# A block of four transformer layers: dummy products for TensorE, a new order of the first steps, and a shorter normalisation on GpSimd

## The chip, the cores and the metric

The kernel runs on one core of a Trainium2 chip. A core has five engines that run side by side and meet through semaphores: PE (TensorE, matrix products and transposes into PSUM), DVE (VectorE), ACT (ScalarE, table functions and scaled copies), POOL (GpSimd) and SP (SyncE, which here issues nearly all DMA transfers). PEld is the loading of a product's stationary operand. The metric is the device time of one execution in microseconds (us); lower is better. The time before is 1635.87 us, the median of three runs (1634.98 to 1640.96).

## The reference, cut to what matters

The input x has 128 sequences of 64 tokens with 128 channels in float32, with one condition vector of 128 channels per sequence and a context of 64 tokens per sequence. Four layers follow each other; the change touches the start of the first one and the normalisation of all.

```python
def _ln(x):
    mu = jnp.mean(x, axis=-1, keepdims=True)
    var = jnp.var(x, axis=-1, keepdims=True)
    return (x - mu) * jax.lax.rsqrt(var + EPS)
...
# layer 0
mod = jax.nn.silu(t_emb) @ adaln_w + adaln_b
sh_sa, sc_sa, g_sa, sh_ff, sc_ff, g_ff = jnp.split(mod[:, None, :], 6, axis=-1)
xm = _ln(x) * (1.0 + sc_sa) + sh_sa
qkv = (xm @ qkv_w + qkv_b).reshape(B, N, 3, H, HD)      # 16 heads of 8
...
x_sa = _attend(q, k, v) @ sa_proj_w + sa_proj_b         # softmax(q k / sqrt(8)) v
x = x + g_sa * x_sa
...                                                     # cross attention to the context, then an MLP
x = x + g_ff * x_ff
```

Layer 1 is a cross attention, layer 2 again self attention, cross attention and MLP, and layer 3 a small attention to the context with a gated mixture of three experts.

## The kernel before, in words

The 8192 tokens are held on the chip as 16 groups of 512 (`xs[s]`, 128 partitions x 4 x 128); a group is 8 sequences. All weights and groups are loaded once by SP in the order in which the program names them (L76 to L117). The order of the instructions on each engine is written out by hand (`stages`); no scheduler moves anything.

An attention runs over the 16 groups in half steps: step `k` computes the scores of half `k%2` of group `k//2`. I number the score products by their step: scores 0 and 1 are those of group 0, scores 2 and 3 of group 1, and so on. One step on PE is: scores of this step (`sc`, L470), transposes of the last step's shifted scores (`pp`, L495), products of the step before that with the values (`po`, L512), and between them pieces of the preparation of later groups and the finish of earlier ones. On DVE a step is a maximum over the scores (`mx`, L477) and their difference to it (`e`, L479); ACT takes the exponential (`eT`, L499). There is one PSUM tile for the scores, so scores k+1 wait until `e` of step k has read it.

`prepare` is the preparation of one group, cut by `yield` into pieces; `ahead_1(i)` runs the next piece of group i. For self attention the pieces are: (1) nothing, (2) mean and variance on DVE (L312, L314) and 1/sqrt on POOL (`rs`, L321 and L322, a power), (3) the normalised `xn` (`normed_by_pool`: a negated mean `nmu` on POOL at L361, then four instructions at L364, on POOL, for the first group on DVE), (4) transposes on PE (`psT`, L334) and the modulation `xm` (eight instructions, one per sequence: for the first group on DVE at L349, otherwise on ACT at L351), (5) nothing, (6) the keys (`pk` L428, `kT` L430) and their copies masked by head (`kbd`, L436, on POOL, for the first group on DVE), (7) the queries (`pq` L441, `qT` L443), (8) the values (`pvv` L451) into a block tile `vbd` (L456, L457). Two `vbd` tiles are cleared once on POOL by `clear` (L171 to L173).

`condition` transposes the condition (`pc`, L245), takes its silu on ACT (`scT`, L247, with a load of ACT's function table ahead of it) and transposes the bias rows (`pv`, L249, `vec`, L250). `first_mods` are three lists of products for the six modulation tables (`pm` L195, additions L199). In the MLPs the modulation is made by `modulated`: one multiplication of the whole tile on DVE (L339) and one addition on POOL (L340), ahead of the first MLP product (`ph`, L675). `first_tables` makes a table of gates (`gb` L219, `pg` L224, `gate_rows` L225, a DMA at L226) and a folded bias (`bvs` L233, `pb` L237, L238). Small PSUM tiles come from the pool `mm`, which has two buffers.

Of the kernel before, what the change touches and what calls it, by code (L numbers as in the profile page):

```python
# [9 lines left out]
F32 = mybir.dt.float32  # L10
AF = mybir.ActivationFunctionType
ALU = mybir.AluOpType
# [3 lines left out]
P = 128  # L16
NST = 16
TT = 4
NB = 8
L = 64  # L20
# [39 lines left out]
def tile_kernel(ctx: ExitStack, tc: tile.TileContext, a: dict, out: bass.AP):  # L60
    nc = tc.nc
    V, S, G, T = nc.vector, nc.scalar, nc.gpsimd, nc.tensor
# [3 lines left out]
    def const(shape, name):  # L66
        return cp.tile(shape, F32, tag=name, name=name)

    x_d = a["x"].rearrange("b n c -> (b n) c").rearrange("(s t p) c -> s p t c", t=TT, p=P)
# [2 lines left out]
    out_d = out.rearrange("b n c -> (b n) c").rearrange("(s t p) c -> s p t c", t=TT, p=P)  # L72


    cond = const([P, P], "cond")
    nc.sync.dma_start(cond, a["cond_1024"])  # L76
    vec_rows = const([_NVEC, P], "vec_rows")
# [13 lines left out]
                nc.sync.dma_start(t, src.rearrange("(k p) n -> p k n", p=P))  # L91
                w[name] = t

    xs = [const([P, TT, P], f"x{s}") for s in range(NST)]

    def load_groups(which):
        for s in which:
            nc.sync.dma_start(xs[s], x_d[s])

    load_groups((0,))  # L100
    load_weights(("L0_xcond_adaln", "L0_xcond_qkv"))
    load_groups((1,))
    load_weights("L0_xcond_sa")
# [3 lines left out]
    for name, n in (("L0_xcond_ca_proj_b", P), ("L1_xcond_bp", P), ("L2_xcond_b_cproj", P), ("L3_xcond_router_b", 3)):  # L107
        t = const([P, n], name)
# [11 lines left out]
    make_identity(nc, ident)  # L120
    nhalf = const([P, TT], "nhalf")
    G.memset(nhalf, -0.5)

    stack, attention_stack = ExitStack(), ExitStack()
    dp = ctx.enter_context(tc.tile_pool(name="dp", bufs=1, space=bass.MemoryType.DRAM))
# [34 lines left out]

    def mm(name):
        return pools[1].tile([P, 512], F32, tag="mm", name=name)

# [4 lines left out]
    def clear(t):  # L170
        G.memset(t, 0.0)  # L171
        G.memset(t[0:L, :, :, 16:17], 1.0)
        G.memset(t[L:P, :, :, 17:18], 1.0)  # L173
# [69 lines left out]
    def condition():  # L243
        pc = mm("pc")
        T.transpose(pc[:, :P], cond, ident)  # L245
        V.tensor_copy(condT, pc[:, :P])
        S.activation(scT, pc[:, :P], AF.Silu)  # L247
        pv = mm("pv")
        T.transpose(pv[:, :_NVEC], vec_rows, ident[:_NVEC, :_NVEC])  # L249
        V.tensor_copy(vec, pv[:, :_NVEC])  # L250
        V.tensor_scalar_add(vec1, vec, 1.0)

    first_mods = modulations("L0_xcond_adaln_w", "L0_xcond_adaln_b", 6, (1, 4))
# [41 lines left out]
    def mod(name, i, s):  # L295

        return mods[name][:, i, ts(s, NB)].unsqueeze(2).broadcast_to([P, NB, L])

    def by_batch(t):
        return t.rearrange("p (b l) -> p b l", b=NB)  # L300
# [29 lines left out]
    def transposed(psum, src):  # L330

        ps = psum.tile([P, 512], F32, tag="mm", name="psT")
        for t in range(TT):
            T.transpose(ps[:, ts(t, P)], src[:, t, :], ident)  # L334
        return ps

    def modulated(pool, ps, name, scale, shift, s, tag="xm"):
        xm = pool.tile([P, NT], F32, tag=tag, name=tag)
        V.tensor_tensor(by_batch(xm), by_batch(ps), mod(name, scale, s), ALU.mult)  # L339
        G.tensor_tensor(by_batch(xm), by_batch(xm), mod(name, shift, s), ALU.add)  # L340
        return xm

    def modulated_by_batch(pool, ps, name, scale, shift, s, tag="xm", by_dve=False):
        xm = pool.tile([P, NT], F32, tag=tag, name=tag)
        for b in range(NB):
            k = NB * s + b
            m, p = (mods[name][:, i, k : k + 1] for i in (scale, shift))
            if by_dve:
                V.tensor_scalar(xm[:, ts(b, L)], ps[:, ts(b, L)], m, p, ALU.mult, ALU.add)  # L349
            else:  # L350
                S.activation(xm[:, ts(b, L)], ps[:, ts(b, L)], AF.Identity, bias=p, scale=m)  # L351
        return xm


# [2 lines left out]


    def normed_by_pool(pool, src, mv, rs, tag, engine=G):
        nmu = pool.tile([P, TT], F32, tag="nmu" + tag, name="nmu")  # L360
        G.tensor_scalar(nmu, mv[:, :, 0], -1.0, 0.0, ALU.mult, ALU.add)  # L361
        xn = pool.tile([P, TT, P], F32, tag=tag, name=tag)
        for t in range(TT):
            engine.tensor_scalar(  # L364
                xn[:, t, :], src[:, t, :], nmu[:, t : t + 1], rs[:, t : t + 1], ALU.add, ALU.mult
            )
        return xn

# [9 lines left out]
    def prepare(pools, at):  # L378

        pool, psum = pools[:2]  # L380
        s, layer = at["s"], at["layer"]
        eps = 1e-5 if layer == "L1c" else 1e-6
        cross = layer[2] == "c"
        if cross:
            c = pool.tile([P, TT, P], F32, tag="c", name="c", bufs=3)
            nc.sync.dma_start(c, ctx_d[s])
        yield
        if layer == "L1c":
            mv = x_mv[:, s]
            rs = inv_std(pool, mv, eps)  # L390
        else:
            mv, rs = stats_of(pool, xs[s], eps)
        yield
        xn = normed_by_pool(pool, xs[s], mv, rs, "xn", V if at.get("first") else G)
        if cross:
            cn = c
            if layer != "L0c":
                cn = pool.tile([P, TT, P], F32, tag="cn", name="cn", bufs=1)
                for t in range(TT):
                    rs, nb = (v[eps][:, s, t : t + 1] for v in (ctx_rs, ctx_nb))  # L400

                    if layer == "L1c":
                        G.tensor_scalar(cn[:, t, :], c[:, t, :], rs, nb, ALU.mult, ALU.add)
                    else:
                        S.activation(cn[:, t, :], c[:, t, :], AF.Identity, bias=nb, scale=rs)
        yield
        if layer == "L1c":
            kv_in = modulated_by_batch(pool, transposed(psum, cn), "L1_xcond_Wss_kv", 0, 1, s, "cm")
        elif cross:
            kv_in = copied(pool, transposed(psum, cn), "cm")  # L410
            if layer == "L0c":
                nc.sync.dma_start(ctxT[s], kv_in)
        else:
            q_in = kv_in = modulated_by_batch(
                pool, transposed(psum, xn), at["wmod"], 1, 0, s, by_dve=at.get("first", False)
            )
        yield
        if not cross:
            pass
        elif layer == "L1c":  # L420
            q_in = modulated(pool, transposed(psum, xn), "L1_xcond_Wss_q", 0, 1, s)
        else:
            q_in = copied(pool, transposed(psum, xn), "xm")
        yield


        pk = psum.tile([P, 512], F32, tag="mm", name="pk")
        T.matmul(pk, at["wk"], kv_in, start=True, stop=True)  # L428
        kT = pool.tile([P, NT], F32, tag="kT", name="kT")
        S.activation(kT, pk, AF.Identity, bias=at["bk"])  # L430
        i = turn[0] % 2
        turn[0] += 1
        vbd = vbds[i]
        kbd = pool.tile([P, 4, NB, L], F32, tag="kbd", name="kbd")
        for j in range(4):
            (V if at.get("first") else G).tensor_scalar(  # L436
                kbd[:, j], by_batch(kT), mask[:, j : j + 1], 1.0, ALU.mult, ALU.mult
            )
        yield
        pq = psum.tile([P, 512], F32, tag="mm", name="pq")  # L440
        T.matmul(pq, at["wq"], q_in, start=True, stop=True)  # L441
        qT = pool.tile([P, NT], F32, tag="qT", name="qT")
        S.activation(qT, pq, AF.Identity, bias=at["bq"])  # L443
        at.update(qT=qT, kbd=kbd)
        yield

        wv_pair = at["wv"].rearrange("p (i j d) -> p j i d", j=2, d=HD)
        pvv = psum.tile([P, NB, L], F32, tag="mm", name="pvv")
        for b in range(NB):
            for j in range(2):  # L450
                T.matmul(  # L451
                    pvv[ts(j, L), b, :], kv_in[:, ts(b, L)], wv_pair[:, j],
                    start=True, stop=True,
                )
        pv4 = pvv.rearrange("p b (i d) -> p b i d", d=HD)
        S.copy(vbd[0:L, :, :, 0:HD], pv4[0:L])  # L456
        S.copy(vbd[L:P, :, :, HD : 2 * HD], pv4[L:P])  # L457
        at["vbd"] = vbd
# [712 lines left out]

    def stages():
        ats = [attention_of(s, layer) for layer in ("L0s", "L0c") for s in groups]
        ats[0]["first"] = True
        ahead_1, steps_1 = attend(pools, ats)
        ahead_2, steps_2 = attend(
            pools, [attention_of(s, layer) for layer in ("L1c", "L2s", "L2c") for s in groups]
# [33 lines left out]
            return turns[last - 1 :]  # L1211


        clear(vbds[0])
        ahead_1(0, 1, 2, 3)
        condition()
        ahead_1(0, 0)
        first_mods[0]()
        ahead_1(0, 0, 1, 2, 0, 0, 1)
        psum_for_attention()  # L1220

        steps_1[0]([lambda: ahead_1(2), lambda: clear(vbds[1]), lambda: ahead_1(1, 1, 0, 3)])
        tables = first_tables()
        steps_1[1]()
        first_mods[1]()
        steps_1[2]()
        for f in tables[:3]:
            f()
        steps_1[3]((), tables[3:])
        for f in steps_1[4:6]:  # L1230
            f()
        first_mods[2]()
        n = last + 2 + len(heads_0)
        for f in steps_1[6:-n]:
# [38 lines left out]
    with tc.manual_schedule():  # L1273
        stages()
# [30 lines left out]
```

## Time and profile before

| | |
|---|---|
| median of three runs | 1635.87 us |
| the profiled execution, its own time | 1636.9 us |
| its span, first to last instruction | 1635.1 us |
| PE busy | 1581.5 us, 97% of the span |
| DVE, POOL, ACT busy | 1296.4, 1079.4, 1038.6 us |
| PE busy in the stretches 0-20, 20-40, 40-60 us | 11.14, 15.78, 18.55 us |
| PE busy in 60-80 us and in 460-520 us | 19.48 of 20, 60.0 of 60 us |
| `nmu` (L361) | 128 instructions on POOL, median 0.193 us |
| `xn` (L364) | 508 on POOL, mean 0.452 us |

Times in a profile are microseconds from the start of the span, unless marked ns. A group row or timeline row gives start, duration, engine, line, operation, output tile and inputs; a float32 product appears as two passes on PE (a count of x2 is one product). The chain is followed back from the last instruction: at each step to what released it, or to the instruction before it on its engine. A busy PE is not PE at its peak: matrix products are pipelined and their ends are modelled.

### The profile page before, as it was taken

To read this page: it belongs to the slowest core of one execution; us is meant where nothing else is said; L and a number is where in the kernel's file an instruction comes from. 1 tells how busy PE (TensorE), PEld (TensorE's weight loads), DVE (VectorE), ACT (ScalarE), POOL (GpSimd) and SP (SyncE) were. 2 spreads that over 40 slices of the span, in tenths; PEclk is the share of its full clock that TensorE was granted. 3 is DMA by queue.
4 is the path that set the end of the run, shared out by engine and by line. 5 is a ranking of instruction groups with operands and counts; after the bars stand their busy time and mean duration, and the time that the engine had idled before them with its cause. 6 is when DMAs were issued, how large, how long until landed. Compare 5 with 4: busy or idle time off the path is not lost.

```text
span 1635.1 us, 64936 instructions
## 1 busy us (share of the span) xinstructions
PE 1581.5 (97%) x27842; PEld 1090.9 (67%) x27842; DVE 1296.4 (79%) x2430; ACT 1038.6 (64%) x1714; POOL 1079.4 (66%) x1814
## 2 busy tenths in 40 slices
PE   6999999998999899999999999998999999999998
PEld 4677767776554467777777677776777666666665
DVE  6999989999566688899999999998454566666666
ACT  5778767776333587788887888886334544444443
POOL 5688777775899888986787786665876333333322
PEclk9999999999999999999999999999999999999999
DMA  7333443322202012211333432221432111111100
GB/s 208 82 93 85 109 118 87 93 81 60 62 27 58 27 47 72 63 47 47 95 86 92 102 99 62 72 56 53 125 91 77 31 37 40 39 34 33 36 11 20
DMA packets 146783, 112.71 MB, mean 69 GB/s; under 512 B 36357, under 2 KB 125247, under 8 KB 146495
## 3 DMA queue, kind: packets, MB, share of 16 engines
q1 hardware_dynamic: 146288, 108.53, 25.0%
q8 instruction: 219, 3.59, 0.9%
q14 instruction: 69, 0.57, 0.1%
q10 hardware_dynamic: 207, 0.03, 0.0%
HBM read 83.99 MB, written 14.02 MB: 60 GB/s over the span
## 4 chain that ended last, share of the span: by engine, by line
PE 79%; DVE 13%; ACT 3%; POOL 2%; issue 1%; DMA 1%; SPq 1%; POOLq 0%; DVEq 0%
PE sc L470 9%; PE pp L495 9%; PE po L512 7%; PE ph L1062 6%; PE ph L675 6%; PE ph L1063 6%; DVE mx L477 5%; DVE e L479 5%; PE po L1093 5%; PE psT L334 5%; PE pk L428 5%; PE py L554 4%; PE py L691 3%; PE pvv L451 3%; PE pq L441 3%; PE py L681 2%
## 5 line engine op out<-in xcount | busy, mean ns | idle before, releaser
L499 ACT ACTIVATE eT<-pp 128x1024 f32<-128x1024 f32 x320 | 329.8, 1030 | 162.5 <-PE pp L495 162.5
L477 DVE TENSOR_REDUCE mx<-sc 128x32 f32<-128x2048 f32 x160 | 366.6, 2291 | 61.8 <-PE sc L470 61.8
L479 DVE TENSOR_TENSOR e<-sc,mx 128x2048 f32<-128x2048 f32 x160 | 366.6, 2291 | 5.4
L495 PEld LDWEIGHTS pp<-ident,e 64*128 64x128 f32 x5120 | 185.1, 139 | 142.6 <-ACT eT L499 46.7
L436 POOL TENSOR_SCALAR kbd<-kT,mask 128x512 f32<-128x512 f32 x316 | 212.4, 689 | 44.0 <-ACT kT L430 41.2
L495 PE MATMUL pp<-ident,e 64*128 64x64 f32 x5120 | 228.9, 229 | 8.4 <-DVE e L479 4.7
L364 POOL TENSOR_SCALAR xn<-x,nmu,rs 128x128 f32<-128x128 f32 x508 | 223.0, 452 | 13.3
L548 POOL TENSOR_TENSOR oT<-o,rb 128x512 f32<-128x512 f32 x80 | 102.0, 1275 | 153.1 <-DMA rb<-recs 65.8
L470 PE MATMUL sc<-kbd,qT 32*64 32x256 f32 x5120 | 181.7, 391 | 16.2 <-DVE e L479 15.3
L676 ACT ACTIVATE h<-ph,vec 128x512 f32<-128x512 f32 x128 | 87.4, 688 | 153.1 <-PE ph L675 152.9
L512 PE MATMUL po<-eT,vbd 128*32 128x64 f32 x10240 | 178.6, 222 | 1.2 <-issue 1.2
L1069 ACT ACTIVATE h<-h 128x512 f32<-128x512 f32 x112 | 70.5, 630 | 148.0 <-DVE h L1065 129.1
L512 PEld LDWEIGHTS po<-eT,vbd 128*32 128x32 f32 x10240 | 152.1, 110 | 14.0 <-issue 1.7
L322 POOL TENSOR_TENSOR rs<-rs,nhalf 128x4 f32<-128x4 f32 x128 | 130.3, 1018 | 10.6
L470 PEld LDWEIGHTS sc<-kbd,qT 32*64 32x64 f32 x5120 | 98.3, 132 | 53.5 <-DVE e L479 19.3
L1065 DVE TENSOR_TENSOR h<-ph,ab 128x512 f32<-128x512 f32 x112 | 77.0, 688 | 55.7 <-PE ph L1063 55.5
L312 DVE BATCH_NORM_STATS2 st<-x 128x6 f32<-128x128 f32 x512 | 110.5, 278 | 0.6
L1098 DVE SCALAR_TENSOR_TENSOR acc<-po,pr,acc 128x128 f32<-128x128 f32 x192 | 67.3, 350 | 44.1 <-PE po L1093 39.5
L1062 PE MATMUL ph<-nx,w 128*128 128x512 f32 x192 | 99.9, 602 | 0.0
L520 ACT COPY o<-po 128x512 f32<-128x512 f32 x160 | 95.7, 598 | 5.7 <-PE po L512 3.5
L1063 PE MATMUL ph<-u,w_ev 128*128 128x512 f32 x192 | 98.0, 592 | 0.0
L1093 PEld LDWEIGHTS po<-w_2o,h 128*128 128x128 f32 x768 | 92.1, 192 | 8.7 <-issue 8.4
(261 smaller groups left out, 2851.8 us busy)
## 6 DMA issues: line engine op xcount, KB each, us to landing
rb<-recs SPq DMA_DIRECT2D x80, 256.0 KB
c<-in_ctx_dram SPq DMA_DIRECT2D x64, 256.0 KB
o<-o SPq DMA_DIRECT2D x320, 32.0 KB
gt<-gate_L_xcond_sa_proj_w SPq DMA_DIRECT2D x32, 256.0 KB
gt<-gate_L_xcond_W_proj SPq DMA_DIRECT2D x32, 256.0 KB
gt<-gate_L_xcond_W_mlp SPq DMA_DIRECT2D x32, 256.0 KB
x<-in_x_dram SPq DMA_DIRECT2D x16, 256.0 KB
ctxT<-cm SPq DMA_DIRECT2D x16, 256.0 KB
```

The costliest lines, as they stand in the source:

```text
L322: G.tensor_tensor(rs, rs, nhalf, ALU.pow)
L364: engine.tensor_scalar(xn[:, t, :], src[:, t, :], nmu[:, t : t + 1], rs[:, t : t + 1], ALU.add, ALU.mult)
L436: (V if at.get("first") else G).tensor_scalar(kbd[:, j], by_batch(kT), mask[:, j : j + 1], 1.0, ALU.mult, ALU.mult)
L470: T.matmul(sc[ts(h, L), g, ts(t2, 256)], qT[ts(g, 32), ts(b, L)], kbd[ts(g, 32), :, b, :], start=True, stop=True,)
L477: V.tensor_reduce(mx, sc.rearrange("p g (m k) -> p (g m) k", k=L), AX.X, ALU.max)
L479: V.tensor_tensor(e, sc.rearrange("p g (m k) -> p (g m) k", k=L), mx.unsqueeze(2).broadcast_to([P, 32, L]), ALU.subtract,)
L495: T.transpose(pp[:, h, ts(4 * g2 + 2 * i + t2, L)], e6[ts(h, L), 2 * gg + g2, t2, i], ident[ts(h, L), ts(h, L)],)
L499: S.activation(eT[:, gg], pp, AF.Exp, scale=HD ** -0.5)
L512: T.matmul(po[ts(g, 32), i, ts(2 * t2 + h, L)], at["vbd"][:, 4 * u + 2 * t2 + h, 2 * g + i, :], e7[:, g // 2, h, g % 2, i, t2, :], start=T ...
L1062: T.matmul(ps, wn, d["nx"], start=True, stop=False)
L1063: T.matmul(ps, we, d["u"], start=False, stop=True)
L1093: T.matmul(po[:, ex, :], d[q][:, ts(t, P)], k3["w_2o"][:, q, :], start=r == 0, stop=r == 1)
```

## The change

The change has these parts.

- **Dummy products.** A tile `busy` of ones is set on DVE. `keep_busy(n)` multiplies it with itself n times into a tile that nothing reads. It is called with 8 ahead of everything on PE, with 4 after `condition`, with 2 after the first modulation products, and with 4 after the first group's transposes.
- **First loads.** The first group of x is loaded ahead of the condition on SP's queue.
- **Order of the first steps.** The first group's statistics come ahead of `condition`; the first modulations come ahead of `xn` on DVE; the first `clear` comes after `rs` on POOL.
- **Exponential's table.** An exponential of a 128x4 tile, which nothing reads, follows the silu, so that ACT's table for it is loaded there.
- **Modulation by whole tiles.** For group 0 the eight instructions at L349 become one multiplication and one addition of 128x512, both on DVE; for group 2 the eight at L351 on ACT become a multiplication on DVE and an addition on POOL.
- **Set-up parts spread.** The second list of modulations moves from before step 2 to after it, and the folded bias from step 3 to step 5.
- **Normalisation.** `nmu` is gone in all layers: `xn` is (x - mean) * rs in one instruction, with the mean read from the statistics.

```diff
@@ -72,6 +72,13 @@
     out_d = out.rearrange("b n c -> (b n) c").rearrange("(s t p) c -> s p t c", t=TT, p=P)
 
 
+    xs = [const([P, TT, P], f"x{s}") for s in range(NST)]
+
+    def load_groups(which):
+        for s in which:
+            nc.sync.dma_start(xs[s], x_d[s])
+
+    load_groups((0,))
     cond = const([P, P], "cond")
     nc.sync.dma_start(cond, a["cond_1024"])
     vec_rows = const([_NVEC, P], "vec_rows")
@@ -91,13 +98,6 @@
                 nc.sync.dma_start(t, src.rearrange("(k p) n -> p k n", p=P))
                 w[name] = t
 
-    xs = [const([P, TT, P], f"x{s}") for s in range(NST)]
-
-    def load_groups(which):
-        for s in which:
-            nc.sync.dma_start(xs[s], x_d[s])
-
-    load_groups((0,))
     load_weights(("L0_xcond_adaln", "L0_xcond_qkv"))
     load_groups((1,))
     load_weights("L0_xcond_sa")
@@ -120,6 +120,9 @@
     make_identity(nc, ident)
     nhalf = const([P, TT], "nhalf")
     G.memset(nhalf, -0.5)
+    nhalf2 = const([P, TT], "nhalf2")
+    busy = const([P, P], "busy")
+    V.memset(busy, 1.0)
 
     stack, attention_stack = ExitStack(), ExitStack()
     dp = ctx.enter_context(tc.tile_pool(name="dp", bufs=1, space=bass.MemoryType.DRAM))
@@ -161,6 +164,12 @@
     def mm(name):
         return pools[1].tile([P, 512], F32, tag="mm", name=name)
 
+    def keep_busy(n):
+
+        p = mm("pi")
+        for _ in range(n):
+            T.matmul(p[:, 0:P], busy, busy, start=True, stop=True)
+
 
 
     vbds = [
@@ -245,6 +254,8 @@
         T.transpose(pc[:, :P], cond, ident)
         V.tensor_copy(condT, pc[:, :P])
         S.activation(scT, pc[:, :P], AF.Silu)
+
+        S.activation(nhalf2, nhalf, AF.Exp)
         pv = mm("pv")
         T.transpose(pv[:, :_NVEC], vec_rows, ident[:_NVEC, :_NVEC])
         V.tensor_copy(vec, pv[:, :_NVEC])
@@ -334,21 +345,18 @@
             T.transpose(ps[:, ts(t, P)], src[:, t, :], ident)
         return ps
 
-    def modulated(pool, ps, name, scale, shift, s, tag="xm"):
+    def modulated(pool, ps, name, scale, shift, s, tag="xm", engine=G):
         xm = pool.tile([P, NT], F32, tag=tag, name=tag)
         V.tensor_tensor(by_batch(xm), by_batch(ps), mod(name, scale, s), ALU.mult)
-        G.tensor_tensor(by_batch(xm), by_batch(xm), mod(name, shift, s), ALU.add)
+        engine.tensor_tensor(by_batch(xm), by_batch(xm), mod(name, shift, s), ALU.add)
         return xm
 
-    def modulated_by_batch(pool, ps, name, scale, shift, s, tag="xm", by_dve=False):
+    def modulated_by_batch(pool, ps, name, scale, shift, s, tag="xm"):
         xm = pool.tile([P, NT], F32, tag=tag, name=tag)
         for b in range(NB):
             k = NB * s + b
             m, p = (mods[name][:, i, k : k + 1] for i in (scale, shift))
-            if by_dve:
-                V.tensor_scalar(xm[:, ts(b, L)], ps[:, ts(b, L)], m, p, ALU.mult, ALU.add)
-            else:
-                S.activation(xm[:, ts(b, L)], ps[:, ts(b, L)], AF.Identity, bias=p, scale=m)
+            S.activation(xm[:, ts(b, L)], ps[:, ts(b, L)], AF.Identity, bias=p, scale=m)
         return xm
 
 
@@ -357,12 +365,10 @@
 
 
     def normed_by_pool(pool, src, mv, rs, tag, engine=G):
-        nmu = pool.tile([P, TT], F32, tag="nmu" + tag, name="nmu")
-        G.tensor_scalar(nmu, mv[:, :, 0], -1.0, 0.0, ALU.mult, ALU.add)
         xn = pool.tile([P, TT, P], F32, tag=tag, name=tag)
         for t in range(TT):
             engine.tensor_scalar(
-                xn[:, t, :], src[:, t, :], nmu[:, t : t + 1], rs[:, t : t + 1], ALU.add, ALU.mult
+                xn[:, t, :], src[:, t, :], mv[:, t, 0:1], rs[:, t : t + 1], ALU.subtract, ALU.mult
             )
         return xn
 
@@ -411,9 +417,13 @@
             if layer == "L0c":
                 nc.sync.dma_start(ctxT[s], kv_in)
         else:
-            q_in = kv_in = modulated_by_batch(
-                pool, transposed(psum, xn), at["wmod"], 1, 0, s, by_dve=at.get("first", False)
-            )
+            first = at.get("first", False)
+            if first or at.get("second", False):
+                q_in = kv_in = modulated(
+                    pool, transposed(psum, xn), at["wmod"], 1, 0, s, engine=V if first else G
+                )
+            else:
+                q_in = kv_in = modulated_by_batch(pool, transposed(psum, xn), at["wmod"], 1, 0, s)
         yield
         if not cross:
             pass
@@ -1171,7 +1181,7 @@
 
     def stages():
         ats = [attention_of(s, layer) for layer in ("L0s", "L0c") for s in groups]
-        ats[0]["first"] = True
+        ats[0]["first"] = ats[2]["second"] = True
         ahead_1, steps_1 = attend(pools, ats)
         ahead_2, steps_2 = attend(
             pools, [attention_of(s, layer) for layer in ("L1c", "L2s", "L2c") for s in groups]
@@ -1211,24 +1221,30 @@
             return turns[last - 1 :]
 
 
+        keep_busy(8)
+        ahead_1(0, 1, 2, 3)
+        ahead_1(0)
+        condition()
+        keep_busy(4)
+        first_mods[0]()
+        keep_busy(2)
+        ahead_1(0)
         clear(vbds[0])
-        ahead_1(0, 1, 2, 3)
-        condition()
-        ahead_1(0, 0)
-        first_mods[0]()
-        ahead_1(0, 0, 1, 2, 0, 0, 1)
+        ahead_1(0)
+        keep_busy(4)
+        ahead_1(0, 1, 2, 0, 0, 1)
         psum_for_attention()
 
         steps_1[0]([lambda: ahead_1(2), lambda: clear(vbds[1]), lambda: ahead_1(1, 1, 0, 3)])
         tables = first_tables()
         steps_1[1]()
+        steps_1[2]()
         first_mods[1]()
-        steps_1[2]()
         for f in tables[:3]:
             f()
-        steps_1[3]((), tables[3:])
-        for f in steps_1[4:6]:
-            f()
+        steps_1[3]((), tables[3:4])
+        steps_1[4]()
+        steps_1[5]((), tables[4:])
         first_mods[2]()
         n = last + 2 + len(heads_0)
         for f in steps_1[6:-n]:
```

## The prediction

> **What bounds the kernel now.** I read the busy shares first, then PE's busy time and clock by stretch, then the chain of waits from the start, then PE's waits.
>
> ```profile
> PE 1581.5 (97%) x27842; PEld 1090.9 (67%) x27842; DVE 1296.4 (79%) x2430; ACT 1038.6 (64%) x1714; POOL 1079.4 (66%) x1814
> ```
> ```profile
> 0.00:20.00 20.00, 11.14 (x82) 6.04 (x82) 11.41 (x46) 4.01 (x8) 11.51 (x28) 1.00 0.92 242
> 20.00:40.00 20.00, 15.78 (x326) 10.45 (x324) 15.77 (x28) 16.26 (x35) 11.63 (x22) 0.91 0.68 183
> ...
> 60.00:80.00 20.00, 19.48 (x482) 13.99 (x482) 18.95 (x20) 16.54 (x33) 16.66 (x27) 1.00 0.38 96
> ```
>
> PE is idle 54 us in all (1635.1 - 1581.5), and 14.5 of these lie in the first 60 us (20-11.14, 20-15.78, 20-18.55). From 60 us on the first attention runs at its own pace: scores start at 62.84, 68.83, 74.77, 80.76, so 5.97 us a step, in which PE's own work and the loop scores, `mx`, `e` (1.12 + 2.29 + 2.29 and the hand-overs) are both nearly full. The change can therefore gain at the start, and what it gains there is carried to the end unless a later stall absorbs it. The chain of waits in the start:
>
> ```profile
> 7.05 0.19 POOL nmu L361
> ...
> 9.02 2.12 DVE xm L349 x8
> ...
> 11.18 2.09 PE pk L428 x2
> ...
> 15.83 2.01 PE sc L470 x32
> ...
> 23.21 2.48 ACT xm L351 x8
> 25.70 1.28 ACT L499
> 27.00 1.03 ACT eT L499
> ...
> 30.14 1.15 PE pm L195 x4
> 31.29 1.92 PE sc L470 x32
> 33.23 2.30 DVE mx L477
> ...
> 43.88 0.44 DVE gate_rows L225
> ```
>
> Three things are to be seen. The first products run at half rate: `pk` takes 2.09 us at 11.18 and 1.12 at 21.45, scores 0 take 2.01 and later ones 1.12. Scores 2 start at 31.29, although `e` of step 1 had left the PSUM tile at 28.94: before them stand the modulation of group 2 and the table load on ACT, which hold the exponential until 27.00 and so the second `pp`, `pvv` and `pm` on PE; the wait was long enough that PE is slow again:
>
> ```profile
> 19.00:29.40 10.40, 6.91 (x126) 1.00 1.04 276
> 29.40:33.00 3.60, 3.60 (x53) 0.53 0.91 252
> ```
> ```profile
> PE ph L675 <- POOL xm L340: 2.5, 3, 1.2
> ```
>
> The columns of the first are stretch, length, PE busy and its instructions, granted clock, DMA share and GB/s. The last is a PE wait outside the start that POOL ends: 2.5 us in three waits, in the MLP of layer 0.
>
> **The change, to the end of scores 0 (17.84 before).** *Dummies.* A dummy is two passes of 128x128; eight such passes took 2.00 us at half rate (`py` at 409.94) and 1.05 at full rate (60.63), so a dummy is about 0.46 or 0.23 us. `busy` is set at about 0.9, so eight dummies fill PE from 1.05 to 4.75 if slow. Their cover: before, PE waited until 3.09 and for the adaln weights until 5.64. The condition now lands behind x, where x landed before (4.38), so `pc` is put off from 3.09 to 4.75. `condT`, `vec` and `scT` (0.29, 0.21, 0.28) end at about 5.85. The next four dummies wait for `vec`, whose PSUM buffer they take, and `pm` stands behind them: the added wait in this step. They end at 7.65 if slow, 6.7 if fast; `pm` could have run at 5.9. Behind `pm` wait the first modulations and now, on DVE, `xn`.
>
> *When does PE get fast?* By the rows, PE became fast in `pvv` at 18.82, 3.0 us after its last pause (15.70), and again at 33.0, 3.6 us of unbroken work after 29.40. [...] But before, `pk` and `pq` were busy 3.8 us from 11.18 to 14.96 and did not do it. So both ends:
> - fast during the four dummies (6.2): `pm` 6.9 to 7.55, modulations (0.61) 8.2, `xn` (1.12) 9.4, `psT` 9.6, `xm` 0.69 + 0.63 by the rows L339 and L559 in place of 2.11, so 11.05; `pk` fast 12.2, `kT` 12.9; DVE must first measure groups 1 and 2 (2.1, as before), so `kbd` (1.68) 13.25 to 14.9; scores 0 end at 16.15: 1.7 us gained. At best (the clock up within the first eight) 2.0.
> - slow until about 11: `pm` ends at 8.6, `xm` at 12.3 (before 11.13, so later), the last four dummies end about there, `pk` is fast; scores 0 end at 17.4: 0.45 gained.
> I take 1.7: eight dummies without a pause are nearest to the rows with 3.0 and 3.6 us.
>
> *Free edits.* The early x lands 0.45 us sooner and `nmu` saves 0.2 + 0.1 us, but `xn` waits for DVE's modulations until 8.2 and `rs` is there at 6.6, so both are hidden. The moved `clear` (2.2 us) lies on POOL at 6.6 to 8.8, ahead of `rs` of group 1, whose variance comes at 12; it would cost only beyond 3 us. SP issues the same transfers, two exchanged; none is moved past another queue. The silent exponential and its load (1.28) lie on ACT at 5.9 to 7.5; ACT is next wanted at 12.2.
>
> **From scores 0 to `mx` 2** (15.39 us before, 17.84 to 33.23). After: `mx`, `e` 4.7; then DVE measures group 3 (1.2) and multiplies for group 2 (0.7), which is new on DVE between two steps and covers scores 1; `mx`, `e` 4.6; scores 2 (1.12) beside the measuring of group 4 (1.25): 12.6 in sum. Is PE ready then? ACT goes from `kT` straight to `eT` (the 2.48 of `xm` and 1.28 of the load are gone), so `pp`, `pq`, `pp`, `pvv` end at about 26, and `pm` has moved; `e` 1 ends at 27.45. Is `kbd` 1? POOL: `rs` of group 3 to 23.5, `kbd` 26.2, then the new addition 1.04 and `xn` of group 3 to 29.1, wanted by PE at 32: covered by 1.2 and 3 us. Gain 2.8, in which the table counts by its row: `xm` ended at 25.69, the load ran 25.70 to 26.98, and `eT` began at 27.00. [...]
>
> **From `mx` 2 to `mx` 6** (24.94 before). `pb` no longer waits for `gate_rows` (44.36 against 43.75, where scores 4 could go): 0.7 gained at `mx` 4. The folded bias (0.34 on PE) and its addition (0.29) now stand with the third modulations ahead of scores 6: 0.6 lost there. Sum 0, from -0.7 to +0.7.
>
> **`nmu` elsewhere.** 128 x (0.193 + about 0.1 to the next start) is 37 us of POOL, nearly all of it where PE or DVE bounds. At the MLP of layer 0 POOL runs without a pause (`xm` L340 at 427.05 and 434.88: 7.83 us a turn), and PE waits for it 1.18, 0.69 and about 0.6 us. One, two and one `nmu` of 0.29 go ahead of these: at most 1.1, at least 0.3 if the waits move; I take 0.6. That subtracting costs POOL what adding a negated mean did is not shown by a row; the nearest is `cn` (L403, other operations, 1.74 for four against 1.73), so I take no difference.
>
> **Sum.** 1.7 + 2.8 + 0 + 0.6 = 5.1 us. The span goes from 1635.1 to 1630.0. The profiled execution took 1636.9, 1.0 over the median; taken off the median, 5.1 us give **1630.8 us**, 0.31% less. About 0.5% (8.2 us) is what a measurement of this kernel can tell from no change, so the forecast lies inside it.
>
> **Rivals.**
> - *The dummies come too late* (PE slow until 11 us and slow again before scores 0, where it idles 1.8 us): 0.45, or -0.5 with slow scores, plus 2.8, and 0.3 for `nmu`: 1633.0. For it: the 3.8 us at 11.18 that did not help. Against it: the dummies are denser.
> - *POOL was worth more*: from 420 to 460 and 520 to 600 us PE is idle 1.9 + 4.8 + 1.7 = 8.4 us. If POOL's shorter turn ends half of that, 4.2 takes the place of 0.6: gain 8.7, 1627.2. For it: POOL without a pause there. Against it: at 545 to 560 PE waits for DVE and `e`, by the chain.
> - *Slower: subtracting is dear on POOL.* In the MLP of layer 0 POOL's turn becomes 7.54 + 4p against PE's 8 x 0.86 + 0.60 + 0.60 + 0.44 = 8.5, p being the extra of one normalisation. It decides from p = 0.24 us. At p = 0.45 (twice today's) 16 turns lose 16 x 0.84 = 13.4; with 4.5 gained, +8.9: 1644.8. Against it: the equal row L403.
> - *Nothing arrives*: the start is gained, but the stalls behind transfers at 200 to 235 us (PE idle 1.5 us) and the slow spells at 407 and 559 us fall differently: 1636.
>
> **How the numbers follow.** The forecast 0.52; dummies late 0.18; POOL worth more 0.18; nothing arrives 0.06; dear subtraction 0.06. Faster by over 0.5% (below 1627.7): most of the third and a little of the first, 0.22; slower (above 1644.0): most of the last, 0.05; within: 0.73. The range holds the first two with the start's ends (gain 2.5 to 7) and most of the third and fourth: 1625.0 to 1637.5.
>
> **What would show it.** `pk` of group 0 at 1.1 us and scores 0 ending near 16.2; no table load after 8 us; scores 2 at about 27.5, granted clock 1.0 from 20 to 33; scores 7 at about 58.4 instead of 62.84; POOL's `xn` at 0.43 to 0.45 us and PE's waits for L340's successor below 2.5. It would be wrong if scores 7 gained under 3 us, or if the gain at 60 us isn't found again at 400.

## The result and the profile after

The changed kernel takes **1663.31 us** (median; 1662.45 to 1665.17), the kernel before 1637.09 us beside it: a ratio of **1.016**, 95% interval 1.014 to 1.018. It is slower by 26 us, where I forecast 1630.8 us (range 1625.0 to 1637.5) and gave "slower" 0.05. The profiled execution took 1662.45 us, with a span of 1660.7 (before 1635.1).

The busy times of the page after, then the group of the normalisation in its list of costliest groups (behind the count: busy us, mean ns of one, and the engine's idle time before it):

```profile
PE 1595.6 (96%) x27878; PEld 1098.8 (66%) x27878; DVE 1297.0 (78%) x2426; ACT 1036.8 (62%) x1707; POOL 1240.5 (75%) x1687
...
L370 POOL TENSOR_SCALAR xn<-x,mv,rs 128x128 f32<-128x128 f32 x444 | 353.6, 807 | 0.0
```

POOL was to get shorter by 37 us and is busy 161 us longer (1079.4 before). One normalising instruction takes 807 ns (mean) where it took 452. The stretches that I had read before (behind the length: busy us of PE, PEld, DVE, ACT and POOL, PE's granted clock, DMA share, GB/s), and PE's longest wait in the kernel after (us in total, times, longest):

```profile
0.00:20.00 20.00, 14.96 (x89) 11.10 (x90) 11.50 (x42) 4.48 (x7) 10.54 (x21) 0.93 0.86 228
20.00:40.00 20.00, 17.16 (x310) 11.29 (x310) 14.98 (x27) 13.55 (x28) 17.06 (x25) 0.81 0.73 197
60.00:80.00 20.00, 19.66 (x508) 14.08 (x498) 18.93 (x20) 16.50 (x33) 19.31 (x24) 1.00 0.42 93
```
```profile
PE ph L685 <- POOL xm L351: 16.8, 16, 2.2
```

PE's 14.96 in the first stretch holds the dummies (before 11.14). In 60 to 80 us POOL is now busy 19.31 of 20 (before 16.66). The wait for `xm` in the MLPs grew from 2.5 us in 3 to 16.8 in 16.

Where the 25.6 us of span came from is seen by following the same instruction through the kernels (start in us; e1 is the changed kernel with the old normalisation, e2 the kernel before with the new one, both below):

| instruction | before | after | after - before | e1 | e2 |
|---|---|---|---|---|---|
| scores 7 | 62.84 | 63.86 | +1.0 | 59.23 | 62.65 |
| first `ph` of the MLP of layer 0 | 412.5 | 413.7 | +1.2 | 408.8 | 411.4 |
| last group's `py` of that MLP | 548.9 | 565.6 | +16.7 | 545.6 | 565.5 |
| first `ph` of the MLP of layer 2 | 1140.2 | 1158.4 | +18.2 | 1136.5 | 1158.6 |
| last `ph` of that MLP | 1269.6 | 1293.5 | +23.9 | 1265.8 | 1293.6 |
| end of the span | 1635.1 | 1660.7 | +25.6 | 1631.4 | 1659.2 |

The MLP of layer 0 gives 15.5 us of the loss, the MLP of layer 2 5.7. The new start, which was to gain, is 1.0 us later at scores 7. These columns are one execution each, and the start is not the same in all: e6 and e7 below, which change nothing ahead of the MLP of layer 0, have scores 7 at 61.34 and 61.12, where the profile before has 62.84.

POOL's row of the MLP of layer 0, kernel before and then kernel after:

```profile
451.40 1.75 POOL L364 TENSOR_SCALAR xn<-x,nmu,rs 128x128 f32<-128x128 f32 x4
453.11 1.04 POOL L340 TENSOR_TENSOR xm<-xm,mod_L_xcond_adaln_w 128x512 f32<-128x512 f32 x1
...
459.23 1.75 POOL L364 TENSOR_SCALAR xn<-x,nmu,rs 128x128 f32<-128x128 f32 x4
460.94 1.04 POOL L340 TENSOR_TENSOR xm<-xm,mod_L_xcond_adaln_w 128x512 f32<-128x512 f32 x1
```
```profile
454.98 3.14 POOL L370 TENSOR_SCALAR xn<-x,mv,rs 128x128 f32<-128x128 f32 x4
458.09 1.04 POOL L351 TENSOR_TENSOR xm<-xm,mod_L_xcond_adaln_w 128x512 f32<-128x512 f32 x1
...
463.95 3.15 POOL L370 TENSOR_SCALAR xn<-x,mv,rs 128x128 f32<-128x128 f32 x4
467.07 1.04 POOL L351 TENSOR_TENSOR xm<-xm,mod_L_xcond_adaln_w 128x512 f32<-128x512 f32 x1
```

From one `xm` to the next a turn is 7.83 us before and 8.98 after: four normalisations cost 1.40 more, and `nmu` saves 0.29. There is no pause on POOL in either.

### The profile page after: what moved, and what is told of

Read it like the earlier page. It is cut to its first block, busy times and chain, and to the rows that moved or that the text cites. A ratio compares the mean times of both kernels' runs of the same rounds, so it can differ in the third digit from the quotient of the medians.

```text
span 1660.7 us, 64840 instructions
## 1 busy us (share of the span) xinstructions
PE 1595.6 (96%) x27878; PEld 1098.8 (66%) x27878; DVE 1297.0 (78%) x2426; ACT 1036.8 (62%) x1707; POOL 1240.5 (75%) x1687
## 4 chain that ended last, share of the span: by engine, by line
PE 67%; DVE 11%; POOL 10%; DMA 4%; ACT 4%; SPq 2%; issue 2%; POOLq 0%; DVEq 0%
PE sc L480 8%; PE pp L505 8%; PE po L522 6%; PE ph L1072 6%; PE ph L1073 6%; PE po L1103 5%; DVE mx L487 5%; DVE e L489 4%; POOL xn L370 4%; PE py L564 4%; PE pk L438 4%; PE psT L345 4%; PE ph L685 4%; PE pvv L461 3%; PE pq L451 3%; PE py L701 2%
## 5 line engine op out<-in xcount | busy, mean ns | idle before, releaser
L370 POOL TENSOR_SCALAR xn<-x,mv,rs 128x128 f32<-128x128 f32 x444 | 353.6, 807 | 0.0
L480 PE MATMUL sc<-kbd,qT 32*64 32x256 f32 x5120 | 180.1, 388 | 15.2 <-DVE e L489 11.6
L1096 POOL TENSOR_SCALAR g<-g 128x512 f32<-128x512 f32 x16 | 9.9, 620 | 127.2 <-ACT g L1095 127.2
```

Source lines behind the costliest of these rows:

```text
L370: engine.tensor_scalar(xn[:, t, :], src[:, t, :], mv[:, t, 0:1], rs[:, t : t + 1], ALU.subtract, ALU.mult)
L480: T.matmul(sc[ts(h, L), g, ts(t2, 256)], qT[ts(g, 32), ts(b, L)], kbd[ts(g, 32), :, b, :], start=True, stop=True,)
```

## The experiments

The times are read against runs of the kernel before on the same chip: 1636.98 us for e1 to e4, 1634.94 for e5 to e8, 1636.96 for e9 and e10. Executions of one kernel lie up to 6 us to either side of their median, so a median that differs by 1 us is told with its interval or not used.

### e1: the changed kernel with the old normalisation

```diff
-                xn[:, t, :], src[:, t, :], mv[:, t, 0:1], rs[:, t : t + 1], ALU.subtract, ALU.mult
+                xn[:, t, :], src[:, t, :], nmu[:, t : t + 1], rs[:, t : t + 1], ALU.add, ALU.mult
```

with `nmu` on POOL ahead of it, as before.

> The changed kernel with the old normalisation: the negated mean on POOL and then four additions. Theory S (subtraction is dear on POOL, and nothing else of the change costs): the normalisation on POOL is back at 0.45 us from 0.80, the MLP of layer 0 loses its 15.6 us, and what is left is the gain of the start: 1632 to 1635, against 1637 before. Rival theory (the new start or the spread parts cost as well): 1640 or more.

Measured: 1635.03 us, ratio 0.9991 (0.9981 to 1.0001). The 28 us are gone, and what remains is the rest of the change. Its profile is 3.6 us ahead at scores 7 and keeps this to the end (3.7 of span); against the starts of e6 and e7 it is 2.1 and 1.9 ahead, which is what the medians give. Its normalising group:

```profile
L372 POOL TENSOR_SCALAR xn<-x,nmu,rs 128x128 f32<-128x128 f32 x508 | 224.6, 456 | 13.3
```

### e2: the kernel before with the subtraction only

```diff
-        nmu = pool.tile([P, TT], F32, tag="nmu" + tag, name="nmu")
-        G.tensor_scalar(nmu, mv[:, :, 0], -1.0, 0.0, ALU.mult, ALU.add)
-                xn[:, t, :], src[:, t, :], nmu[:, t : t + 1], rs[:, t : t + 1], ALU.add, ALU.mult
+                xn[:, t, :], src[:, t, :], mv[:, t, 0:1], rs[:, t : t + 1], ALU.subtract, ALU.mult
```

> The kernel before with one edit: the negated mean is gone and the normalisation subtracts. Theory S: the whole loss and more, since the start's gain is missing: 1663 to 1668. Rival theory (the start costs as well): below 1660.

Measured: 1660.84 us, ratio 1.0148 (1.0131 to 1.0164). One edit makes nearly all of the loss. The waits of PE in its profile:

```profile
PE ph L673 <- POOL xm L340: 19.1, 17, 3.7
```

The time lies between my two expectations (1663 or more, or below 1660) and so decides for neither of them as they were put. The last column of the table above shows the loss in place: +16.6 at the end of the MLP of layer 0, +24 at the end. At scores 7 e2 is level with the profile before, but 1.3 and 1.5 us behind e6 and e7, so it seems that the subtraction cost something in the old start too. In the new one scores 7 come 4.6 us later than without it (63.86 after, 59.23 in e1); not all of this is the subtraction's, as the last part shows.

### e3: the changed kernel with an addition in place of the subtraction

```diff
-                xn[:, t, :], src[:, t, :], mv[:, t, 0:1], rs[:, t : t + 1], ALU.subtract, ALU.mult
+                xn[:, t, :], src[:, t, :], mv[:, t, 0:1], rs[:, t : t + 1], ALU.add, ALU.mult
```

> The changed kernel with an addition in place of the subtraction, the mean still read from the statistics: it computes x plus the mean, so the sign of the mean is left out; its time shows what the missing negation alone is worth. Theory S: the operation is what is dear, so the normalisation takes 0.45 us, and the time is that of the kernel with the negated mean less 0.3 to 1.5 us: 1631 to 1634. Rival theory (the scalar read with a stride from the statistics is what is dear): 0.80 us and 1660 or more.

Measured: 1634.79 us, ratio 0.9989 (0.9978 to 1.0000); `xn` takes 460 ns in the mean (456 in e1). (This kernel adds the mean where it should be taken off, so only its time is of use.) The operand that is read with a stride out of the statistics is not what costs; the subtraction is. This kernel has POOL's turn as the change meant it: 7.58 us from `xm` to `xm` in the MLP of layer 0, against 7.86 in e1, and that MLP is 1.0 us shorter (135.8 against 136.8). The gain lies in its last two groups, whose first `ph` follow each other after 7.96 and 9.41 us where e1 has 8.93 and 9.67; in the middle of the MLP both kernels have the same turns, 7.74 and 7.97, which are PE's own (see e6). So `nmu` was worth about 1 us there, and in the medians nothing that can be measured.

### e4: e1 without the 18 dummy products

```diff
-        keep_busy(8)
-        keep_busy(4)
-        keep_busy(2)
-        keep_busy(4)
```

> The changed kernel with the old normalisation and without the 18 dummy products. If the dummies are worth what was forecast (1.7 us to the end of scores 0), it is slower than the same with dummies by 1.5 to 2 us. If the half rate of the first products is paid back by the modulation products that no longer wait behind dummies, the two are within 1 us; scores 0 end at about 17.0 in both.

Measured: 1636.42 us, ratio 0.9998 (0.9987 to 1.0008); scores 7 at 60.83 against 59.23. In the two profiles the dummies are worth 1.6 us; the medians differ by 1.4, within their intervals.

### e5: a price list for POOL

At the end of the kernel before stand three instructions of each kind, on tiles that nothing reads any more. This kernel ran once; only its rows are used.

```diff
+        for _ in range(3):
+            G.tensor_scalar(free[:, :128], given[:, :128], nhalf[:, 0:1], nhalf[:, 1:2], ALU.subtract, ALU.mult)
...
```

> The kernel before with a price list at its end: on POOL, three instructions each of tensor_scalar at 128x128 with add-mult, subtract-mult, mult-subtract, mult-add (scalars from a tile), subtract-mult and add-mult at 128x64 and 128x512, the same two at 128x128 with constants for scalars, tensor_tensor of 128x512 with add, subtract, mult; and on DVE add-mult and subtract-mult at 128x128. Their results are read by nothing. If the subtraction itself is dear (per element), subtract-mult takes about 0.80 us at 128x128 against 0.45, also in this place where DVE and PE have little to do, mult-subtract is dear too, and the difference grows with the width: about 0.18 at 128x64 and 1.4 at 128x512. If it is a fixed price of another code for the operation, the difference is about 0.35 at every width. If the price comes from other engines' traffic in the layers, subtract-mult costs 0.45 here. A tensor_tensor subtract costs as much as an add if only the form with scalars is dear. DVE: no difference (0.34).

The groups of that stretch by line. L1275, L1277, L1279 and L1281 are add-mult, subtract-mult, mult-subtract and mult-add; L1283 and L1289 subtract-mult and add-mult at 64 columns, L1285 and L1287 the same at 512; L1291 and L1293 the two with constants; L1295 and L1297 are a tensor_tensor add and subtract:

```profile
L1285 POOL TENSOR_SCALAR x<-x,nhalf 128x512 f32<-128x512 f32 x3 | 6.2, 2076 | 0.3
L1297 POOL TENSOR_TENSOR x<-x,x 128x512 f32<-128x512 f32 x3 | 3.8, 1262 | 0.2
L1295 POOL TENSOR_TENSOR x<-x,x 128x512 f32<-128x512 f32 x3 | 3.8, 1262 | 0.2
...
L1279 POOL TENSOR_SCALAR x<-x,nhalf 128x128 f32<-128x128 f32 x3 | 2.4, 799 | 0.3
L1277 POOL TENSOR_SCALAR x<-x,nhalf 128x128 f32<-128x128 f32 x3 | 2.4, 799 | 0.3
L1287 POOL TENSOR_SCALAR x<-x,nhalf 128x512 f32<-128x512 f32 x3 | 2.3, 772 | 0.3
L1293 POOL TENSOR_SCALAR x<-x 128x128 f32<-128x128 f32 x3 | 1.9, 644 | 0.2
L1283 POOL TENSOR_SCALAR x<-x,nhalf 128x64 f32<-128x64 f32 x3 | 1.8, 585 | 0.3
...
L1281 POOL TENSOR_SCALAR x<-x,nhalf 128x128 f32<-128x128 f32 x3 | 1.4, 452 | 0.3
L1275 POOL TENSOR_SCALAR x<-x,nhalf 128x128 f32<-128x128 f32 x3 | 1.4, 452 | 0.2
L1289 POOL TENSOR_SCALAR x<-x,nhalf 128x64 f32<-128x64 f32 x3 | 1.2, 396 | 0.3
L1291 POOL TENSOR_SCALAR x<-x 128x128 f32<-128x128 f32 x3 | 0.9, 299 | 0.3
```

A subtraction in a tensor_scalar on POOL costs by the column: from 64 to 512 columns subtract-mult grows from 585 to 2076 ns, 3.33 ns a column, and add-mult from 396 to 772, 0.84 ns a column. It is the same first or second (799 both), with a tile's scalars or with constants (0.347 and 0.345 us more), and with nothing beside it on DVE, which is idle for 35.57 us there, or on PE, which has no instruction from 1636 us on. A tensor_tensor subtracts at the price of an addition (1262 ns both). DVE makes no difference: three of either kind took 1.11 us.

Of the 772 ns of add-mult at 512 columns, 430 are the columns at 0.84 ns each; the other 342 are a fixed part, which the 64 columns show too (396 less 54).

### e6 and e7: POOL's time in the MLP of layer 0, without a subtraction

```diff
         def norm(d):
+            if not by_token:
+                for _ in range(1):
+                    G.tensor_scalar(
+                        more, ident, nhalf[:, 0:1], nhalf[:, 1:2], ALU.add, ALU.mult
+                    )
             d["xn"] = normed_by_pool(pool, xs[d["s"]], d["mv"], d["rs"], "xn")
```

and in e7 `range(3)`.

> The kernel before, with one more POOL instruction (add and mult, 128x128, about 0.43 us, result read by nothing) ahead of each normalisation in the MLP of layer 0; no subtraction anywhere. If POOL's turn of 7.83 us was already the length of a turn there (PE's own work, from start to start, is 7.74 and not the 8.5 of my prediction), each of some 14 turns gets longer by 0.43 to 0.45: +6, so 1643, and the MLP takes 145.5 us in place of 139.5. If PE's turn is 8.5, the extra 0.43 is hidden: 1637 to 1638, and the loss of the changed kernel in that MLP has another cause than POOL's time.

> As the run with one more POOL instruction, but with three (about 1.29 us a turn, near the 1.14 by which the subtraction lengthens POOL's turn). If the time of a turn is POOL's: 14 times 1.29 is +18, so 1655, the MLP 157.5 us. If PE's turn of 8.5 stood above it: POOL 9.12 against 8.5, 16 times 0.62 is +10, so 1647.

Measured: e6 1641.87 us, ratio 1.0044 (1.0028 to 1.0059); e7 1655.93 us, ratio 1.0134 (1.0116 to 1.0152). The waits of PE, first e6, then e7:

```profile
PE ph L681 <- POOL xm L341: 6.0, 7, 1.8
```
```profile
PE ph L681 <- POOL xm L341: 18.9, 12, 2.8
```

| kernel | POOL's turn | longer than before by | MLP of layer 0 (first `ph` to the last group's `py`) | longer by | turns that this makes |
|---|---|---|---|---|---|
| before | 7.83 | | 136.3 | | |
| e6 | 8.30 | 0.47 | 142.5 | 6.2 | 13 |
| after | 8.98 | 1.15 | 151.8 | 15.5 | 13.5 |
| e7 | 9.42 | 1.59 | 158.3 | 21.9 | 13.8 |
| e2 | 8.98 | 1.15 | 154.1 | 17.8 | 15.5 |

Every added tenth on POOL is paid in 13 to 14 turns, whatever the instruction is; only e2 lies above. Its excess is all between the first `ph` of the second group and that of the third, which takes 12.64 us there and 10.08 before, and from 9.30 to 12.64 in the eleven kernels followed here. Without this stretch e6, after, e7 and e2 lose 5.6, 15.2, 20.3 and 15.2 us: 12 to 13 turns, and e2 as much as after. Nothing besides POOL's time is needed to explain what the subtraction did there, and there is no slack: the first 0.47 is already paid in full. e7 came out above my 18 because each extra instruction takes 0.53 of the turn, with the gap to the next, and not 0.43.

Why there is no slack is in PE's timeline of the kernel before:

```profile
454.67 1.02 PE L675 MATMUL ph<-xm,L_xcond_fc_w 128*128 128x512 f32 x2
455.53 1.02 PE L681 MATMUL py<-h,L_xcond_fc_w 128*128 128x512 f32 x2
...
458.11 0.60 PE L334 MATMUL psT<-ident,xn 128*128 128x128 f32 x4
458.54 1.02 PE L675 MATMUL ph<-xm,L_xcond_fc_w 128*128 128x512 f32 x2
...
461.98 0.60 PE L714 MATMUL psB<-ident,y 128*128 128x128 f32 x4
462.41 1.02 PE L675 MATMUL ph<-xm,L_xcond_fc_w 128*128 128x512 f32 x2
...
468.01 0.38 PE L237 MATMUL pb<-L_xcond_Wp,bvs 128*128 128x128 f32 x2
```

From 454.67 to 462.41 PE does a whole group without a pause: eight products of 0.86 from start to start and two sets of transposes of 0.43, 7.74 us. The next group, up to 470.38, holds a set-up product for a later layer besides (`pb`) and takes 7.97, and so on by turns: 7.86 in the mean. POOL's 7.83 was already as long.

### e8: e1 without the early table

```diff
-        S.activation(nhalf2, nhalf, AF.Exp)
```

> The changed kernel with the old normalisation (as in the first of these runs) and without the silent exponential, so that ACT loads the exponential's table at its first real use. If the load of 1.28 us stands on the path, the maximum of step 2 comes up to 1.3 us later than the 28.8 us with the early table (30.1), and scores 7 at 60.5 in place of 59.2: 1636.3 against 1635.0. If the difference of step 1 on DVE bounds that stretch anyway, nothing changes: 28.8, 59.2, 1635.0.

Measured: 1634.37 us, ratio 0.9999 (0.9987 to 1.0011); the maximum of step 2 at 28.72 (28.79 in e1). The load moved and cost nothing. ACT's timeline in e8:

```profile
21.04 0.69 ACT L440 ACTIVATE kT<-pk,vec 128x512 f32<-128x512 f32 x1 [0.18 <-PE pk L438]
21.74 1.28 ACT L509 ACT_TABLE_LOAD   x1
23.32 1.02 ACT L509 ACTIVATE eT<-pp 128x1024 f32<-128x1024 f32 x1 [0.29 <-PE pp L505]
```

The load is over at 23.02, and the exponential still waits 0.29 for its transposes. Before, the load stood behind the eight modulations of group 2, which are now gone from ACT.

### e9 and e10: the negated mean on DVE, and fewer dummies

e9 is e1 with this line; e10 also leaves out the dummies after the condition and after the first modulation products.

```diff
-        G.tensor_scalar(nmu, mv[:, :, 0], -1.0, 0.0, ALU.mult, ALU.add)
+        V.tensor_scalar(nmu, mv[:, :, 0], -1.0, 0.0, ALU.mult, ALU.add)
```

> The changed kernel with the addition of a negated mean as before, but the negated mean made on DVE, so that POOL has the shorter turn that the change was after, without the dear operation. POOL's turn in the MLP of layer 0 is then 7.54 against PE's 7.74 and the MLP 138.9 us in place of the 140.0 of the kernel with both on POOL: 1.0 to 1.3 gained over that one, 1634 where it gave 1635.0; against before 2 to 3 us. If DVE's instruction waits for a buffer that POOL's additions free, or delays the maximum and the difference in the attentions (0.15 us each, 48 steps at most where DVE is nearly full): 0 to -4, so 1635 to 1639.

> As the kernel with the negated mean on DVE, without the four dummies after the condition and the two after the first modulation products (twelve of 18 are left). Those six stand ahead of the modulation products or of the transposes and did not get PE fast before 10.4 us in the changed kernel: without them the modulation products start up to 1.6 us earlier, the end of scores 0 comes 0 to 1.0 earlier than 15.8, and the time is 1633 to 1634. If they are what makes PE fast at scores 0, these take 2.0 in place of 1.1 and the time is 1635.

Measured: e9 1641.86 us, ratio 1.0036 (1.0022 to 1.0049); e10 1640.5 us, ratio 1.0023 (1.0014 to 1.0032). Both lose, and lie above all that I had expected. The MLP of layer 0 does get shorter (136.1 and 136.0 against 136.8), but scores 7 start near 63.2, 4 us later than in e1. Of these, 1.5 are there at scores 0 already (16.15 and 16.09 against 14.63), since PE was slow early on: in e9 the four dummies after the condition took 2.08 us, in e1 1.16, and in e10 the modulation products 1.20, in e1 0.68. PE's waits and POOL's timeline in e9:

```profile
PE sc L482 <- DVE nmu L369: 5.0, 2, 3.2
```
```profile
16.47 1.74 POOL L372 TENSOR_SCALAR xn<-x,nmu,rs 128x128 f32<-128x128 f32 x4
22.32 1.73 POOL L372 TENSOR_SCALAR xn<-x,nmu,rs 128x128 f32<-128x128 f32 x4 [4.11 <-DVE st L323]
```

For the rest, two things are to be seen. PE runs at half clock again (scores 1 take 2.01 us, in e1 1.12). And POOL stands 4.11 us idle ahead of the second `xn`, whose `nmu` ran at 21.90 on DVE, behind the maximum and the difference of step 0. POOL's `clear` and keys stand behind it. In e1 that `xn` began at 17.26. How much each takes was not separated. The profile of e9 is its slowest run, and loses 5 us more than that of e10 up to the MLP of layer 0 (first `ph` at 418.1 and 413.1); this was not traced. In e10 scores 0 start at 16.09, in e9 at 16.15, so leaving out the six dummies moved nothing there; the two medians are within their spread of each other, and whether those six are worth anything is not settled.

## Why the prediction was wrong, point by point

**The step that failed** is the sentence on the operation in the part on `nmu`: "That subtracting costs POOL what adding a negated mean did is not shown by a row; the nearest is `cn` (L403, other operations, 1.74 for four against 1.73), so I take no difference". The row I leaned on has neither a subtraction in it nor another price, so it said nothing of the new operation. The runs show 0.80 in place of 0.45 us for one normalisation; e3 takes the operand out of the question, e5 the neighbours.

**The rival that held** is "Slower: subtracting is dear on POOL". Its mechanism, place and POOL's side were right: 7.54 + 4p is 8.94 at p = 0.35, and the turn measured 8.98. Its other side, "PE's 8 x 0.86 + 0.60 + 0.60 + 0.44 = 8.5", was wrong twice over: the transposes' 0.60 is a modelled duration that overlaps the next product, 0.43 from start to start, and set-up products add 0.23 to every other turn, not 0.44 to each. With 7.86 the point from which it decides is p = 0.08, not 0.24, and the price at p = 0.35 in that MLP is about 15.5 us where the formula with 8.5 gives 16 x 0.44 = 7. I had the fact in hand: in the kernel before, `xm` followed `xm` at 7.83 us without a pause, which with a PE turn of 8.5 could not have gone on for nine turns. PE's wait of only 2.5 us, which I took for no more than the bound of a gain, was the sign of a tie.

The other losses I had not placed. In the MLP of layer 2 PE waited for POOL nowhere before, and 4.4 us in four waits after: late in that MLP a turn of POOL is 10.43 us where it was 7.96. Between and after the two MLPs 1.5 and 1.7 us more were lost, which I have not traced. In the start, the two normalisations at 16.23 took 6.25 us where e1 has 3.8. PE there, in the kernel after and then in e1:

```profile
17.87 0.48 PE L345 MATMUL psT<-ident,xn 128*128 128x128 f32 x1 [0.42 <-POOL xn L370]
...
22.47 2.07 PE L438 MATMUL pk<-xm,L_xcond_qkv_w 128*128 128x512 f32 x2 [0.66 <-ACT xm L359]
24.34 1.06 PE L345 MATMUL psT<-ident,xn 128*128 128x128 f32 x4
25.33 2.01 PE L480 MATMUL sc<-kbd,qT 32*64 32x256 f32 x32
```
```profile
19.95 1.13 PE L440 MATMUL pk<-xm,L_xcond_qkv_w 128*128 128x512 f32 x2 [1.49 <-ACT xm L359]
21.03 0.63 PE L345 MATMUL psT<-ident,xn 128*128 128x128 f32 x4
21.59 1.12 PE L482 MATMUL sc<-kbd,qT 32*64 32x256 f32 x32
```

Scores 2 start 4.63 us later after than in e1 (32.21 against 27.58), and this comes in four parts. Scores 0 end 1.28 later (17.03 against 15.75), mostly because the four dummies were slow (2.08 us against 1.16); that is not the subtraction's doing. From there PE waits for each part of `xn` (0.42, 0.30 and 0.31 us), and `pk` begins 1.24 later. Then the products run at half clock (granted 0.50 from 17.5 to 26 us, 1.00 in e1), which takes 1.22 up to scores 1 and 0.89 in them. The profile names `xn` of group 3 as what scores 2 waited for, but they begin 0.15 us after `e` of step 1 has ended, as they do in e1, where no `xn` ends there; so the new addition and that `xn` did not hold them back. The half clock came in this stretch in both kernels that subtract (`pk` took 2.07 us in each), but in e9 too, where PE had waited no longer from scores 0 to `pk` than in e1 (1.48 and 1.49), and in e10: in these two, `mx` of step 1, which waits for scores 1, starts 2.01 us after DVE's `xm` of group 2, which waits for the transposes ahead of scores 1 (1.12 in e1). It did not come in e1, e3, e4 or e8 (`pk` 1.12 or 1.13 us). Whether the waits for `xn` bring it on stays open.

**The rest of the forecast, by e1.** Without the subtraction the kernel takes 1635.03 against 1636.98 us, a gain of 2.0 in the medians, at the edge of what can be told from none, and 3.7 in the profile, where I had 5.1.
- *To the end of scores 0*: predicted 16.15, measured 15.75; the four dummies after the condition were fast (1.16 us) as I had assumed. This is not certain from run to run: in the profile of the changed kernel the same four took 2.08, and scores 0 ended at 17.03.
- *From scores 0 to `mx` 2*: predicted 12.6, measured 13.04 (28.79 - 15.75), a gain of 2.35 for the predicted 2.8. But 1.6 of it is not the new order's. I had read PE's slow spell before scores 2 as a part of the old order ("the wait was long enough that PE is slow again"); in e6 and e7 the same wait of 2.16 us stands there, PE stays fast behind it (granted clock 1.00 from 29.4 to 33.0 us, where it was 0.53), and the stretch takes 13.8 us instead of 15.39. The new order is worth 0.8 here. I also counted the load of the table, and e8 shows that this part was free: without the modulations ahead of it on ACT, the load is hidden. PE's row of the slow spell's stretch in e6, where it did not come:

```profile
29.40:33.00 3.60, 3.60 (x128) 1.00 0.88 237
```

- *From `mx` 2 to `mx` 6*: predicted 0 (from -0.7 to +0.7), measured -0.8: 25.77 in place of 24.94. The gain at `mx` 4 was 0.88 (0.7 predicted), the loss at `mx` 6 0.87 (0.6 predicted). Missing in my sum was the other half of the moved modulations: their products and additions (0.60 on DVE), and the row bias behind them, now stand between steps 2 and 3, and `mx` 3 follows `mx` 2 after 6.73 us where it was 5.90. I had booked their leaving and not their arriving.
- *`nmu` elsewhere*: 0.6 predicted; e3 gives 1.0 in the MLP of layer 0. In the middle of that MLP it can't give anything, since PE's own turns, 7.86 in the mean, were as long as POOL's 7.83. The rival in which POOL was worth much more falls with that.

No version here beats the kernel before by more than can be measured. Of those that compute the reference, the best are e1, 0.9991 (0.9981 to 1.0001), e4 without the dummies, 0.9998, and e8 without the early table, 0.9999.

## What to carry to other kernels

When an edit puts a new operation into an inner instruction, its price is unknown until a row with that very operation shows it; a neighbour with other operations is no bound, and the range must hold a doubling. The slack of an engine beside another is read from start to start over a whole turn, of both engines; where both run without a pause, neither has any, however small the wait between them looks. A moved step is booked twice: once where it leaves and once where it arrives. A slow spell that one profile shows is no part of a kernel until a second execution shows it too: here 1.6 of the forecast gain was such a spell.

## What the runs showed of the hardware that I had not expected

- On POOL a tensor_scalar with a subtraction takes 3.33 ns a column, with an addition and a multiplication 0.84 (128x512: 2076 against 772 ns; 128x128: 799 against 452). A tensor_tensor shows no such difference (1262 ns for add, subtract and mult at 128x512), nor does DVE (1.11 us for three of either kind at 128x128).
- With constants in place of a tile's scalars the same instruction on POOL is 0.15 us shorter (add-mult 299 against 452 ns at 128x128, subtract-mult 644 against 799).
- The eight unbroken dummy products from 1.04 us on took 3.78 us (3.79 in e10) in every kernel that has them, where the four from 9.21 us on took 1.06 in e1. The four after the next pause (0.31 us) took 1.16 us in e1, e3 and e8, and 2.08 in the changed kernel and e9, whose products are the same up to there.
- The granted clock of the rows is 1.00 from 0 to 16 us in the kernel before, where `pk` took 2.09 us in place of 1.12. There the products' own durations show the half rate, and this column does not.
